# Four convolution layers on one core: the last three emitted in an explicit order, and loads and stores of the first moved

## The chip, the cores and the metric

The kernel runs on one core of a Trainium2 chip. The metric is the device time of the whole program in microseconds (us). Engines are named as in the profile: PE is TensorE (matmuls), DVE is VectorE, ACT is ScalarE, POOL is GpSimd, SP is SyncE; POOL and SP only issue DMAs here. A float32 matmul shows as two instructions ("passes") on PE.

## The reference, cut to what matters

The input has 32 images of 8 channels and 256 x 256 pixels in float32. Each of four layers adds to x a function of x that was normalized over 4 groups of channels.

```python
x = x + L0(gn(x))      # gn: mean and variance of each image over pairs of channels

def L0(x):
    grid = x
    for _ in range(15):
        mapped = 3.9 * grid * (1 - grid)
        local = conv3x3_per_channel(mapped, K_local)
        grid = 0.85 * (0.7 * mapped + 0.3 * local) + 0.15 * x
    cml = clip(grid, 1e-4, 1 - 1e-4)
    nca = sigmoid(conv1x1(relu(conv3x3(x, Wp, bp)), Wu, bu))          # 8 -> 128 -> 8
    g = sigmoid(conv1x1(relu(conv3x3([x, cml, nca], Wg1, bg1)), Wg2, bg2))   # 24 -> 8 -> 8
    return g * cml + (1 - g) * nca

x = x + conv3x3(quantized(gn(x)), quantized(w1)) / scales + b1   # scale: maximum over all images
x = x + conv3x3(gn(x), w2) + b2
x = x + conv5x5_per_channel(gn(x), w3)
```

## The kernel before, in words

**Two stages.** Layer 1 needs the largest value over the whole batch, so layer 0 is done for all 32 images first, and its sums go to memory (`x1_d`). Then layers 1 to 3 follow for all images.

**Layer 0** weaves two streams of instructions together by hand, inside `tc.manual_schedule()`, where every engine executes in the order in which the program emits (lines 661 to 677). The first stream, `lattice(b)` (L328), does the 15 steps for image b. Six of the eight channels are kept as patches of 16 x 8 pixels on partitions: a patch product and a ring product for the neighbours on PE (L389, L391), an addition on DVE (L400), a square on ACT (L418), and four DMAs that copy the ring (`spread`, L259). Two channels are done on DVE alone (`tap`, L338). A step has two halves of three channels each; the generator says by `yield` how much other work may lie beside each (`BLOCK`). After the last step the patches are turned back (L428), copied to `xb` (L431), and stored to `cr_d` by four GpSimd DMAs (L439).

The second stream, `gated()` (L484), works on the image before. In chunks n of two rows per partition (8 an image), it loads `im` (L501), multiplies (`ph`, L634), applies the rectifier (L639), multiplies into `pn` (L610) and takes the sigmoid to `nh` (L588). A chunk is four batches. A gate (L507) follows some batches later: it loads `xq`, `cq`, their halos and `xc` (L513, L476, L518), multiplies (L526, L534, L538, L543), combines on DVE (L556 to L559), and stores the sum (L564). `due` says in which batch a gate begins; each further piece of it comes one batch later. The driver at L668 takes pieces of `gated` while the lattice's `yield` leaves units for them, and never passes into the next image.

`errands(b)` (L266) holds the DMAs and statistics of the next image, one piece at the end of each half. All loads and stores but those of the rings, the strips and the constants are issued by GpSimd in one order. Statistics are means over partitions by small matmuls (`stats_parts`, L95: products at L104 and L111, copies at L105 and L112); in layer 0 their PSUM tiles come from `ps_c`, three buffers that the lattice uses too, and `held` keeps the gated ones out of the stretch in which a half holds all three. The pool `ps_a` (tag `ps`, three buffers) serves `ph`, `pq` and the transposes.

**Layers 1 to 3** (from L680) are emitted without a manual order: the scheduler of the language orders the instructions from the program's priorities and its own costs. The loop at L830 emits per round b a load of image b, layer 3 of image b-3, layer 2 of b-1, layer 1 of b. Layer 1 quantizes x to bfloat16 `qh` (L743, L704 to L706), copies two halo blocks to `qb` (L143), and makes eight chunks of three products and one with the halo (`conv3`, L726, L730), with ACT, an addition and `bn_stats` after each (L757 to L759). Layer 2 normalizes into `xh` (L765), copies its halo to `xb2`, and does the same in float32 (L774, L775); then it stores to `x3_d` by 16 DMAs (L779), takes statistics (with L133 for a broadcast by group) and loads `y` with rows on partitions (L789). Layer 3 normalizes into `xr` (L797), copies four boundary rows to `xr2` (L803), and for each of four channel pairs and two halves of the rows makes five products (L812), one with the halo (L816) and an addition (L821). The halo product has 128 output columns, of which only the two at the border between the halves are not zero.

Of the kernel before, what the change touches and what calls it, by code (L numbers as in the profile page):

```python
# [17 lines left out]
P = 128  # L18
# [30 lines left out]
BLOCK = 6.5  # L49
# [17 lines left out]
def kernel(  # L67
# [100 lines left out]
    with ExitStack() as es:  # L168
# [97 lines left out]
        def errands(b):  # L266
# [53 lines left out]
            for _ in stats_parts(ps_c, bn, st, gavg_sb, "psc"):  # L320
                yield
            yield

            ps = ps_c.tile([P, 512], F32, name="ps", tag="psc")
# [3 lines left out]
        def lattice(b, ahead):  # L328
# [23 lines left out]
            for t4 in range(TX // 4):  # L352
# [6 lines left out]
                if t4 == 0:  # L359
                    nc.vector.tensor_scalar(  # L360
                        xi, xi, st[:, 0:1], st[:, 1:2], ALU.subtract, ALU.mult
                    )
                if t4 == 1:
# [18 lines left out]
            for step in range(STEPS):  # L382
                for half in range(2):
# [30 lines left out]
                    held.append(half)  # L414
# [7 lines left out]
                    held.clear()  # L422
# [15 lines left out]
            for r in range(0, RB, 4):  # L438
                nc.gpsimd.dma_start(  # L439
                    window(  # L440
                        cr_d[b % 3], r // 4 * C * HB * WP,
                        [[WP, HB * CP], [4 * C * HB * WP, 4], [1, WP]],
                    ),
                    xb[0 : HB * CP, r : r + 4, :],
                )

            row = HB * WP
            for q in range(HB // RQ):
                for c in range(2):
# [7 lines left out]
                    )  # L457

# [22 lines left out]
        held = []  # L481
        place = [0]

        def gated():  # L484
# [22 lines left out]
            def gate(n, quarter):  # L507
# [10 lines left out]
                nc.gpsimd.dma_start(xc, xr_d[b % 3][:, k0 : k0 + 2, :])  # L518
                yield 0
# [49 lines left out]
                parts = stats_parts(ps_c, bn, st, gavr_sb, "psc")  # L569
                more = True  # L570
                while more:

                    if not held:
                        more = next(parts, parts) is None
                    yield 0
# [46 lines left out]
            for n in range(B * NCH):  # L622
# [4 lines left out]
                due.setdefault(batch + 6, []).append(gate(n, quarter))  # L627
# [33 lines left out]
        with tc.manual_schedule():  # L661
# [4 lines left out]
            for b in range(B):  # L666
# [7 lines left out]
                for _ in ahead:  # L674
                    pass
            for _ in rest:
# [3 lines left out]
    with ExitStack() as es:  # L680
# [10 lines left out]
        w3h_sb = const(wt, w3h, [72, 2, P], "w3h_sb")  # L691
# [48 lines left out]
        def layer1(b, x1):  # L740
            for k in range(4):
                t = two.tile([P, 1024], F32, name="tq")
                nc.vector.tensor_scalar(  # L743
                    t, x1[:, bass.ts(k, 1024)], stat1[:, b, 0:1], stat1[:, b, 1:2],
                    ALU.subtract, ALU.mult,
                )
                quantize(
                    qh[:, 4 * k : 4 * k + 4, 1 : 1 + W],
                    t.rearrange("p (r w) -> p r w", w=W), sc[:, 0:1],
                )  # L750
# [224 lines left out]
```

## Time and profile before

The median is 17658.94 us of three runs (17651.33 to 17685.45). The profiled execution spans 17639.8 us.

| part of the profiled execution | us |
|---|---|
| first lattice, alone (L346 of image 0 to L346 of image 1) | 351 |
| lattices 1 to 31, each beside the gated work of the image before | 434 each |
| gated work of the last image, alone, to its last product | about 255 |
| layers 1 to 3, from about 14120 us | about 3520 |
| PE busy, share of the span | 90% |
| DVE busy, share of the span | 66% |

A row of the waits names who waited, for what, the total in us, the number of times and the longest. A row of the timeline has start, duration, engine, line, operation, out<-in and the number merged; in brackets stand the idle time of the engine before it and what ended that. For PE the granted clock matters beside the busy time: at half clock a product takes twice as long and still counts as busy.

### The profile page before, as it was taken

The page shows a single profiled execution, that of the slowest core. Times are in us where ns is not written, and L with a number is a line of the kernel's source. Part 1 is how long each engine was busy: PE and PEld are TensorE (multiplying, and loading weights), DVE is VectorE, ACT ScalarE, POOL GpSimd, SP SyncE. Part 2 cuts the span into 40 slices and gives each one's busy share as a digit, 9 for nine tenths or more (in the row PEclk, how much of TensorE's full clock was granted, in tenths as well). Part 3 has the DMA queues.
Part 4 walks back from the last instruction along what each step waited for, and adds up shares of the span by engine and source line. Part 5 has one row for each costly group of instructions (what it writes and reads, how often), then busy time and mean ns, then how long its engine had stood idle before and what let it go on. Part 6 is the DMA issues. An engine that isn't in the chain of part 4 may idle for free. (4 is left out here: it accounts for less than half of the span.)

```text
span 17639.8 us, 136421 instructions
## 1 busy us (share of the span) xinstructions
PE 15897.8 (90%) x42888; PEld 6371.8 (36%) x42888; DVE 11656.2 (66%) x14652; ACT 5700.9 (32%) x8862; POOL 3931.1 (22%) x6419
## 2 busy tenths in 40 slices
PE   5999999999999999999999999999999977777777
PEld 2333333333333333333333333333333333333333
DVE  6677777777777777777777777777777444444443
ACT  2333333333333333333334333333333410000000
POOL 1222222222222222222222222222222211111111
PEclk7999999999999999999999999999999988888888
DMA  4666666666666666666666666666666644444443
GB/s 95 138 140 140 142 140 139 144 141 141 141 147 140 142 140 143 140 141 144 141 140 146 141 141 141 144 143 141 140 141 133 123 93 89 90 89 89 88 88 81
DMA packets 861103, 2275.97 MB, mean 129 GB/s; under 512 B 296788, under 2 KB 500628, under 8 KB 780388
## 3 DMA queue, kind: packets, MB, share of 16 engines
q0 software_dynamic: 507904, 1492.90, 40.1%
q1 hardware_dynamic: 352484, 774.34, 21.7%
q8 instruction: 350, 5.73, 0.2%
q14 instruction: 365, 2.99, 0.1%
HBM read 1078.68 MB, written 471.38 MB: 88 GB/s over the span
## 5 line engine op out<-in xcount | busy, mean ns | idle before, releaser
L338 DVE SCALAR_TENSOR_TENSOR acc<-strip,taps_sb,acc 128x1024 f32<-128x1024 f32 x3840 | 4929.8, 1284 | 120.4 <-DMA strip<-strip 0.3
L639 ACT ACTIVATE hh<-ph,bp_sb 128x512 f32<-128x512 f32 x4096 | 2763.8, 690 | 5899.1 <-PE ph L634 5839.5
L634 PE MATMUL ph<-im,wp_sb 72*128 72x512 f32 x8192 | 4256.7, 637 | 209.9 <-DMA im<-xn_d 178.8
L400 DVE SCALAR_TENSOR_TENSOR psc<-psc,flat 128x512 f32<-128x512 f32 x2880 | 1934.1, 695 | 3474.3 <-PE psc L391 3459.5
L389 PE MATMUL psc<-state,patch_sb 128*128 128x512 f32 x5760 | 2742.9, 612 | 104.9 <-ACT state L418 62.8
L391 PE MATMUL psc<-rings,ring_sb 80*128 80x512 f32 x5760 | 2641.7, 593 | 26.9 <-DMA rings<-state 26.9
L501 POOL DMA_DIRECT2D im<-xn_d x3072 | 1718.4, 564 | 3695.0 <-PE ph L634 3412.8
L634 PEld LDWEIGHTS ph<-im,wp_sb 72*128 72x128 f32 x8192 | 1542.7, 198 | 2479.2 <-issue 2049.3
L418 ACT ACTIVATE state<-psc,minus 128x512 f32<-128x512 f32 x2688 | 1672.9, 690 | 1423.1 <-DVE psc L400 1309.6
L389 PEld LDWEIGHTS psc<-state,patch_sb 128*128 128x128 f32 x5760 | 1095.4, 195 | 1660.7 <-issue 1312.1
L391 PEld LDWEIGHTS psc<-rings,ring_sb 80*128 80x128 f32 x5760 | 1094.5, 190 | 1425.9 <-issue 1411.7
L610 PE MATMUL pn<-hh,wu_sb 128*32 128x512 f32 x8192 | 1195.9, 642 | 0.6 <-ACT hh L639 0.6
L812 PE MATMUL psv<-xr,w_sb 128*128 128x512 f32 x2560 | 1162.6, 596 | 15.3 <-DVE xr L797 15.3
L526 PE MATMUL pg<-xq,wg_sb 128*128 128x512 f32 x1536 | 809.8, 669 | 276.0 <-DMA xq<-nr_d 276.0
L779 POOL DMA_DIRECT2D x_d<-x x512 | 353.7, 703 | 2612.9 <-DVE x L774 2402.5
L564 POOL DMA_DIRECT2D x_d<-xc x256 | 150.6, 588 | 3171.3 <-DVE xc L559 3154.0
L821 DVE TENSOR_TENSOR y<-psv,y 128x512 f32<-128x512 f32 x256 | 176.8, 691 | 881.9 <-PE psv L816 881.8
L115 ACT ACTIVATE u<-u 128x1 f32<-128x1 f32 x128 | 25.9, 202 | 2264.7 <-DVE u L112 2264.0
L526 PE MATMUL pg<-cq,wg_sb 128*128 128x512 f32 x1536 | 748.9, 626 | 0.0
L726 PE MATMUL psv<-xh,w_sb 128*128 128x512 f32 x1536 | 706.7, 597 | 8.1 <-DVE xh L765 4.1
L812 PEld LDWEIGHTS psv<-xr,w_sb 128*128 128x128 f32 x2560 | 480.5, 190 | 599.9 <-issue 592.1
L338 DVE SCALAR_TENSOR_TENSOR acc<-strip,taps_sb,d 128x1024 f32<-128x1024 f32 x480 | 612.3, 1276 | 0.0
(163 smaller groups left out, 12766.2 us busy)
## 6 DMA issues: line engine op xcount, KB each, us to landing
im<-xn_d POOLq DMA_DIRECT2D x3072, 193.3 KB, 7.8
rings<-state SPq DMA_DIRECT2D x1920, 159.5 KB
rings<-state SPq DMA_DIRECT2D x1920, 106.3 KB
strip<-strip SPq DMA_DIRECT2D x960, 126.0 KB
xn_d<-xb POOLq DMA_DIRECT2D x128, 516.0 KB, 9.0
nr_d<-xb POOLq DMA_DIRECT2D x128, 516.0 KB, 9.8
xq<-nr_d POOLq DMA_DIRECT2D x128, 516.0 KB, 13.3
cq<-cr_d POOLq DMA_DIRECT2D x128, 516.0 KB, 16.1
```

The source lines that it names most:

```text
L338: nc.vector.scalar_tensor_tensor(acc, strip[:, dy : dy + RQ, dx : dx + W], taps_sb[:, 3 * dy + dx : 3 * dy + dx + 1], d2 if dy == 1 and dx ...
L389: nc.tensor.matmul(pss[-1], patch_sb[:, c, :], inner(c), start=True, stop=False)
L391: nc.tensor.matmul(pss[c % HALF], ring_sb[:, c, :], rings[half][:, c % HALF, 0 : TX * SY].rearrange("p (x y) -> p x y", y=SY)[:, :, 0:TY], ...
L400: nc.vector.scalar_tensor_tensor(ps, ps, FLOOR, dr[:, c], ALU.max, ALU.add)
L418: nc.scalar.activation(inner(c), pss[c % HALF], AF.Square, bias=minus)
L501: nc.gpsimd.dma_start(im[24 * dy : 24 * dy + 24, k, 0:run], window(xn_d[b % 3], at, [[HP * WP, C], [1, 3], [1, run]]),)
L526: nc.tensor.matmul(o, wg1_sb[:, s, dx, :], src[:, :, dx : dx + W], start=s == dx == 0, stop=False,)
L610: nc.tensor.matmul(pn[32 * q : 32 * q + 32, :], wu_sb[:, i, :], hh, start=i == 0, stop=i == 3,)
L634: nc.tensor.matmul(ph.rearrange("p (k w) -> p k w", w=W), wp_sb, im[:, :, j * WP : j * WP + W], start=True, stop=True,)
L639: nc.scalar.activation(hh, ph, AF.Relu, bias=bp_sb)
L726: nc.tensor.matmul(o, w[:, dx, :], src[:, 2 * i : 2 * i + 2, dx : dx + W], start=dx == 0, stop=False,)
L812: nc.tensor.matmul(o, w3_sb[:, dx, :], xr[:, k, 2 * g : 2 * g + 2, dx : dx + W], start=dx == 0, stop=False,)
```

## The change

In layers 1 to 3 the order is now written out inside `tc.manual_schedule()`. The layers become generators that give up control after each chunk, and `among` puts small tasks between the chunks. In round b: among layer 3 of image b-3 lie the last statistics of layer 1, normalizing and halo for layer 2 of b-1, and quantizing and halo for layer 1 of b; among layer 2 of b-1 lies normalizing for layer 3 of b-2; among layer 1 of b lie the statistics of layer 2. The point is that each layer's products are preceded by prepared inputs. Layer 3's halo product now has 32 output columns, for the half and the block of partitions that need it, and those of the two halves are emitted one after the other.

In layer 0 the stores of `cr_d` move from the end of a lattice into the next one, a gate's loads begin a batch earlier while its products stay where they were (a second empty `yield`), the statistics' tiles move to the pool `ps_a` and `held` is gone, and `BLOCK` falls from 6.5 to 6.3.

```diff
-BLOCK = 6.5
+BLOCK = 6.3
...
-            for _ in stats_parts(ps_c, bn, st, gavg_sb, "psc"):
+            for _ in stats_parts(psum, bn, st, gavg_sb, "ps"):
...
-            ps = ps_c.tile([P, 512], F32, name="ps", tag="psc")
+            ps = psum.tile([P, 512], F32, name="ps")
             nc.tensor.matmul(ps[:, 0:2], pick_sb, st, start=True, stop=True)
...
+                if t4 == 4 and b > 0:
+                    store(b - 1)
...
-                    held.append(half)
                     yield 1.7
...
-                    held.clear()
                     next(ahead, None)
...
-            for r in range(0, RB, 4):
-                nc.gpsimd.dma_start(
-                    window(
-                        cr_d[b % 3], r // 4 * C * HB * WP,
...
+        def store(b):
+            xb = xbs[b % 2]
+            for r in range(0, RB, 4):
+                nc.gpsimd.dma_start(
+                    window(
+                        cr_d[b % 3], r // 4 * C * HB * WP,
...
                 nc.gpsimd.dma_start(xc, xr_d[b % 3][:, k0 : k0 + 2, :])
                 yield 0
+                yield 0
...
-                parts = stats_parts(ps_c, bn, st, gavr_sb, "psc")
-                more = True
-                while more:
-                    if not held:
-                        more = next(parts, parts) is None
+                for _ in stats_parts(psum, bn, st, gavr_sb, "ps"):
                     yield 0
...
-                due.setdefault(batch + 6, []).append(gate(n, quarter))
+                due.setdefault(batch + 5, []).append(gate(n, quarter))
...
+            store(B - 1)
             for _ in rest:
                 pass
...
-        w3h_sb = const(wt, w3h, [72, 2, P], "w3h_sb")
+        w3h_sb = const(wt, w3h, [72, 2, 32], "w3h_sb")
...
+        def layer3(b, y):
             for g in range(4):
...
                 for k in range(2):
-                    ps = ps_v.tile([P, 512], F32, name="psv")
-                    o = ps.rearrange("p (c w) -> p c w", w=W)
-                    for dx in range(5):
...
+                    pss.append(ps_v.tile([P, 512], F32, name="psv"))
+                    for dx in range(4):
+                        last(k, dx, False)
+                    if k == 0:
+                        yield
+                for k, at in ((0, P - 32), (1, 0)):
                     nc.tensor.matmul(
-                        o, w3h_sb[:, k, :], xr2[:, 2 * g : 2 * g + 2, 0:W],
-                        start=False, stop=True,
-                    )
+                        pss[k][at : at + 32].rearrange("p (c w) -> p c w", w=W), w3h_sb[:, k, :],
+                        xr2[:, mine, 0:W], start=False, stop=False,
+                    )
+                for k in range(2):
+                    last(k, 4, True)
...
-        for b in range(B + 3):
-            if b < B:
-                x1 = load1(b)
-            if b >= 3:
-                layer3(b - 3, *threes.pop(b - 3))
-            if 1 <= b <= B:
-                threes[b - 1] = layer2(b - 1, *twos.pop(b - 1))
-            if b < B:
-                twos[b] = layer1(b, x1)
+        with tc.manual_schedule():
+            x1s[0] = load1(0)
+            for b in range(B + 3):
+                if b + 1 < B:
+                    x1s[b + 1] = load1(b + 1)
+                tasks = {i: [] for i in range(8)}
+                if 1 <= b <= B:
+                    st, parts = sums.pop(1)
+                    for i in range(4):
+                        tasks[i].append(step(parts))
+                    tasks[3].append(lambda: normal2(x2s[b - 1], st))
+                if b < B:
+                    for k, i in enumerate((0, 1, 2, 4)):
+                        tasks[i].append(lambda k=k: quantize1(b, x1s[b], k))
+                    tasks[5].append(lambda: beside(nc.sync, qb, qh, 0))
+                among(layer3(b - 3, ys.pop(b - 3)) if b >= 3 else iter(()), tasks)
+                tasks = {}
+                if 2 <= b <= B + 1:
+                    for g in range(4):
+                        tasks[g] = [lambda g=g: normal3(ys[b - 2], gss[b - 2], g)]
+                    tasks[3].append(beside3)
...
+                among(layer2(b - 1, x2s[b - 1], bn2) if 1 <= b <= B else iter(()), tasks)
+                tasks = {}
+                if 1 <= b <= B:
+                    st3, parts3 = begin(bn2)
+                    for i in range(4):
+                        tasks[i + 1] = [step(parts3)]
...
+                    tasks[6] = [groups]
+                    ys[b - 1] = load3(b - 1)
...
+                among(layer1(b, x1s[b], x2s[b], bn1) if b < B else iter(()), tasks)
+                if b < B:
+                    sums[1] = begin(bn1)
```

## The prediction

> **What bounds the kernel now.** I read the page first, for the stages.
>
> ```profile
> PE 15897.8 (90%) x42888; PEld 6371.8 (36%) x42888; DVE 11656.2 (66%) x14652; ACT 5700.9 (32%) x8862; POOL 3931.1 (22%) x6419
> ...
> PE   5999999999999999999999999999999977777777
> ...
> PEclk7999999999999999999999999999999988888888
> ```
>
> TensorE carries both stages, more tightly in layer 0 (32 slices) than in layers 1 to 3 (the last 8). The view of windows puts numbers on one stretch of each; its columns are busy time by engine, then granted clock, DMA share and GB/s.
>
> ```profile
> 8000.00:10000.00 2000.00, 1900.08 (x5304) 751.57 (x5303) 1474.86 (x1720) 784.20 (x1230) 502.07 (x838) 0.95 0.68 141
> 15000.00:16000.00 1000.00, 765.24 (x1859) 331.15 (x1858) 412.63 (x784) 91.49 (x126) 120.13 (x171) 0.86 0.41 88
> ```
>
> So what can be won is TensorE idle time, and the clock lost with it. Layer 0 first: TensorE's waits between 2000 and 13500 us, some 26.5 images.
>
> ```profile
> PE pg L526 <- DMA xq<-nr_d: 226.0, 26, 9.6
> PE ph L634 <- DMA im<-xn_d: 129.7, 24, 7.1
> PE ps L104 <- ACT state L418: 72.0, 53, 1.4
> ```
>
> The first two come once per image, 8.7 and 5.4 us. One image in TensorE's timeline, then what GpSimd did just before each wait:
>
> ```profile
> 6060.81 1.04 PE L355 MATMUL ps<-eye_sb,flat 128*128 128x128 f32 x8
> 6068.97 3.75 PE L634 MATMUL ph<-im,wp_sb 72*128 72x512 f32 x4 [7.12 <-DMA im<-xn_d]
> ...
> 6138.88 1.98 PE L634 MATMUL ph<-im,wp_sb 72*128 72x512 f32 x4
> 6149.99 4.87 PE L526 MATMUL pg<-xq,wg_sb 128*128 128x512 f32 x6 [9.12 <-DMA xq<-nr_d]
> ```
>
> ```profile
> 6046.87 6.11 POOL L439 DMA_DIRECT2D cr_d<-xb  x4 [10.95 <-DVE xb L431]
> ...
> 6126.57 0.59 POOL L564 DMA_DIRECT2D x_d<-xc  x1 [31.20 <-DVE xc L559]
> ...
> 6129.48 2.19 POOL L501 DMA_DIRECT2D im<-xn_d  x4
> 6134.75 0.60 POOL L513 DMA_DIRECT2D xq<-nr_d  x1 [3.07 <-DMA xn_d<-xb]
> ```
>
> First wait: GpSimd stood 10.95 us at the cr_d stores until VectorE had copied xb, then issued for 6.11 us, and the image loads queued behind. Second: the xq load is issued 8.2 us after GpSimd is released by L564, six im loads ahead of it, and it lands 15 us later. A group of four ph passes takes 3.75 us after the stop against 1.98 us otherwise: the clock is halved. In windows of 10 us the clock reads 0.50 from 6070 to 6090 and 0.87 in the next. Layer 0's clock of 0.95 is 5%, about 22 us of each image's 434 (L346 starts 32 times, first at 34.6 us, last at 13422.8); some 4 of these fall into the waits themselves. The loss is 22 us idle (all waits of that window, about 590 us) and 18 us of half speed; undisturbed, an image would take 434 - 40 = 394 us.
>
> Layers 1 to 3, one round of TensorE:
>
> ```profile
> 15241.10 1.02 PE L730 MATMUL psv<-xb,w_sb 72*128 72x512 f32 x2
> 15244.10 0.58 PE L104 MATMUL ps<-mv,gavr_sb 128*128 128x1 f32 x2 [1.98 <-DVE mv L101]
> 15245.52 0.59 PE L111 MATMUL ps<-t,gavr_sb 128*128 128x1 f32 x2 [0.84 <-DVE t L108]
> 15247.83 0.59 PE L133 MATMUL ps<-sel,ones 128*128 128x8 f32 x2 [1.72 <-DVE sel L131]
> 15253.23 5.70 PE L726 MATMUL psv<-qh,w_bf 128*128 128x512 bf16 x15 [4.80 <-ACT qh L706]
> 15276.33 2.31 PE L730 MATMUL psv<-qb,w_bf 72*128 72x512 bf16 x5 [17.39 <-DMA qb<-qh]
> ```
>
> Layer 2 runs from 15214.46 to 15242.0 without a gap (27.5 us), layer 1 with its waits to 15282.47 (40.5), layer 3 to 15324.30 (41.8): 110 us a round. Layer 1's own 32 bf16 passes are 7 us at the spacing that they show once warm (0.22). The rest of its stretch is a serial chain: statistics of layer 2, quantizing, and 17.4 us for the halo of qh.
>
> **What the Trainium skill says.** *TensorE: Matmul & The Clock Gate*, section "What's actually happening": the clock falls to half after an idle window of about 3.4 us and comes back after about as long a busy one. The trace agrees on the halving; return took 4 us after the 9.12 us wait but about 25 us after the 7.12 us one, so I count clock loss from the trace. The same page, "Architectural detail", calls ScalarE, VectorE and GpSimd strict FIFO, with TensorE moving only weight loads ahead: the GpSimd rows show that. *TensorEngine Tiling (Array Packing)*, "Key Properties": tiles on different partitions compute in parallel. Layer 0's own pair agrees: above and below (L534) start at 6128.98 and 6128.98, two passes each, and L538 follows at 6129.96, 0.98 us for the four.
>
> **The change, part by part.** *Layer 3's halo.* Eight full halo products a round (two passes of 0.43 us, L816 to the next L812: 0.86 us) become four pairs of 32-column products at 0.98: 6.9 - 3.9 = 3.0 us saved. Layer 3 takes 8 x 4.30 (ten L812 passes) + 3.9 + 0.5 for two statistics products = 38.8 us.
>
> *Rounds.* Statistics of layer 1, normalizing, quantizing and both halos now lie inside layer 3. VectorE's work there (8 x 0.69 adds, 4 x 2.24 quantizing, 2.4, about 2 of small ones) is 19 us, inside 39. The xh halo is issued about 23 us into layer 3 and needed at 41 (38.8 + 2.6 of layer 2): 18 us. The trace doesn't show its least duration; the bounds are 7.8 us (what an im load of 193 KB takes to land) and the 17.4 that qb took beside stores, so I count no wait and carry 0 to 4 us. The qb halo has 40 us. Layer 2 stays at 27.5.
>
> *Layer 1's stretch* becomes VectorE's. From layer 2's end: last add, bn_stats and aggregate end at +2.1 (as at 15244.04). Eight chunks at 0.68 + 0.68 plus gaps are 1.44 each, 11.5; statistics pieces among them 2.0; by_group 0.45, then TensorE must answer (0.7) before the copy and the eighth chunk. TensorE waits for the sums at slot 2 (t ready at +5.8) and at slot 6 for sel (+14.7); it issues the last chunk at +15.3, at half clock 1.7 us: 17.0 us. Behind it queues layer 3, which starts cold; I add 2.5 us. Round: 38.8 + 27.5 + 17.0 + 2.5 = 85.8, against 110: 24 us saved. Over 29 full rounds 700; the thinner first and last rounds keep their length within some 20: take 690. Bounds 500 (xh wait of 4, a longer cold start) to 800.
>
> *Layer 0, stores.* The cr_d stores go from the lattice's end to the fifth transpose of the next lattice, when L431 is long done: the 10.95 us of standing goes. The 6.1 us of issue and 1.5 MB of traffic remain, now ahead of the next half's loads, which have roughly 14 us of slack against 3.3 of issue and 7.8 of landing: about 1.5 us stays. Saves 4 us an image (bounds 0 to 5.4).
>
> *Gate loads a batch earlier, the product where it was* (second empty yield). xq goes ahead of six im loads (3.3 us) and of the 3.07 us wait behind them, so it is issued about 7 us earlier: of 8.7 us, 1.7 stay. Saves 7 (4 to 8.7).
>
> *Statistics in the ps pool.* The waits for state L418 (72 + 37.5 + 36.7 us over the window, 5.4 us an image) go. In return the third ph after such a product finds the buffer held until VectorE's copy: of the five products of the image at 6046, the copies end before the third ph in four; only the gated one (product 6197.9, copy until 6204.3) would hold it some 3 us. Net saving 2.5 (-3 to 5).
>
> *BLOCK 6.5 to 6.3.* Lattice gaps go from 229 to 223 units (5+8+9+4+30 x BLOCK+8), the gated work of an image being 223. Both streams still sum to the same TensorE work: nothing, but for the 1.5 us of L428 waits.
>
> *Clock.* With both long stops gone most of the 18 us of half speed goes; shorter stops can still trigger it (a 1.36 us one at 6196 was followed by 0.56 for 10 us). I take 12 saved (4 to 16). Sum: 4 + 7 + 2.5 + 12 = 25.5 us an image, x 31 = 790.
>
> Total: 17658.94 - 690 - 790 = 16180; I say 16200.
>
> **Rivals.** (a) *The stops move*: stores and loads collide at the new place, and clock loss stays. For it: DMA share is 0.9 to 1.0 around 6050 to 6070, the same stretch. Layer 0 then saves about 8 us an image: 17659 - 690 - 250 = 16720. (b) *Layers 1 to 3 stay bound by waits*: the fixed order makes TensorE stand for VectorE's small results and for the xh halo, a round of 98 us: 350 + 790 saved, 16520. Against it: VectorE has idle time for all this (0.41 busy). (c) *Layer 0 runs clean* at 394 us: 40 x 31 + 690, 15730. (d) *Slower*: held ps buffers stop TensorE five times an image for 5 us, half clock for 20 more, +45 x 31 = 1400 less 690 saved: about 18400. Against it: the copies' times above.
>
> **How the numbers follow.** Forecast 0.50, (a) 0.17, (b) 0.14, (c) 0.13, (d) 0.05; something that cancels, 0.01. Range 15800 to 16800: it takes in (a) and (b) and the upper part of the unknowns, and leaves out (d) and most of (c). Faster 0.94, same 0.01, slower 0.05.
>
> **What would show it.** Right: L346 starts every 405 to 412 us; TensorE's waits on im and xq under 2 us an image; no long stop at L439's successor; layer 2 to layer 2 in 84 to 88 us, no wait on qb, and TensorE waiting at L104, L111 and L133 inside layer 1. Wrong: the ph wait turning up against VectorE's st or u copies; a wait of L730 on xb; clock below 0.95 in either stage.

## The result and the profile after

| | us | ratio to before (95% interval) |
|---|---|---|
| before | 17655.14, median beside these runs | |
| after | 16890.31 (16850.15 to 16911.87, four runs) | 0.9561 (0.954 to 0.9583) |

The forecast of 16200 us had the direction right and the size wrong: about 765 us were saved where 1460 were forecast, and 16890 lies above its range. The profiled executions take 17639.8 and 16909.8 us, 730 less. At the last start of L346 (the last image's lattice) they part: it comes at 13373.6 us against 13422.8, 49 us earlier, and from there to the end it takes 3536.2 us against 4217.0, 681 less. That stretch still holds the last lattice and its gated work; from the first product of layer 1 to the end the traces show 2827.4 us against 3489.7, so layers 1 to 3 themselves saved 662. For these the forecast said 690; for layer 0 it said 790. (The 49 is at the low end: two kernels below with the same layer 0, full_halo and s2_stats, reach that start at 13320.4 and 13300.9 us.)

The page of after, first the busy times, then the slices:

```profile
PE 15762.1 (93%) x42888; PEld 6291.4 (37%) x42888; DVE 11707.7 (69%) x14652; ACT 5744.5 (34%) x8862; POOL 3820.6 (23%) x6419
...
PE   5999999999999999999999999999999997999999
...
PEclk7999999999999999999999999999999998999999
```

The last slices have changed from 7 to 9 for TensorE and from 8 to 9 for its clock; nothing is to be seen in the first 32. The view of windows, with the same stretches as before:

```profile
8000.00:10000.00 2000.00, 1899.69 (x5271) 753.50 (x5269) 1460.77 (x1702) 779.64 (x1218) 490.66 (x837) 0.95 0.68 140
15000.00:16000.00 1000.00, 924.66 (x2368) 382.99 (x2367) 546.84 (x1017) 128.04 (x168) 143.84 (x228) 0.94 0.51 114
```

Layer 0 has the same busy time (1899.69 us of 2000 against 1900.08), the same clock and the same DMA share. L346 starts every 433.5 us, before every 433.9 (mean from the third start to the last). Yet the waits are others. TensorE's waits from 2000 to 13000 us, 25.4 images:

```profile
PE ph L633 <- ACT hh L638: 211.7, 103, 4.9
PE psc L393 <- DMA rings<-state: 118.6, 53, 5.9
PE ph L633 <- DMA im<-xn_d: 103.3, 17, 7.6
PE ph L633 <- DVE xb L431: 49.5, 26, 1.9
```

The wait on xq, first before with 226 us, and the one on state L418 are gone. The wait on im fell little: before it was 118.9 us in this stretch, and 48.0 us more of the waits at the same product now stand under other DMAs that landed last. In place of the others stand 8.3 us an image for the rectifier (L638), 4.7 for the lattice's rings, and 1.9 for the copy of xb. The timeline shows the image from 6060 us again, a little later in its own course:

```profile
6067.23 5.46 PE L393 MATMUL psc<-rings,ring_sb 80*128 80x512 f32 x6 [5.56 <-DMA rings<-state]
...
6105.36 2.08 PE L633 MATMUL ph<-im,wp_sb 72*128 72x512 f32 x2 [3.15 <-ACT hh L638]
...
6239.60 3.75 PE L633 MATMUL ph<-im,wp_sb 72*128 72x512 f32 x4 [4.90 <-DMA im<-xn_d]
```

At the head of the image, where TensorE stood 7.12 us for im, it now stands 5.56 us for the rings. In before the ring products of this image came only at 6096.95, 28 us after the im wait, and did not wait. The second row is the new kind of stop. The third is the im wait at a new place. Around the second row, ScalarE:

```profile
6102.85 1.89 ACT L419 ACTIVATE state<-psc,minus 128x512 f32<-128x512 f32 x3 [10.56 <-DVE psc L402]
6104.63 1.84 ACT L638 ACTIVATE hh<-ph,bp_sb 128x512 f32<-128x512 f32 x3
```

and VectorE in the same microseconds:

```profile
6087.65 7.88 DVE L338 SCALAR_TENSOR_TENSOR acc<-strip,taps_sb,acc 128x1024 f32<-128x1024 f32 x6
...
6097.43 0.69 DVE L560 TENSOR_TENSOR cq<-cq,nh 128x512 f32<-128x512 f32 x1
...
6102.12 1.89 DVE L402 SCALAR_TENSOR_TENSOR psc<-psc,flat 128x512 f32<-128x512 f32 x3
```

VectorE has a second half's six taps (7.88 us) and two small instructions to do, then a gate's combination and its statistics (L560 to L567, seven instructions of about 0.69), and only then the additions (L402) of the next half. ScalarE has the squares (L419) that need those additions at the head of its queue and stands 10.56 us; the rectifiers behind them start 0.1 us before the squares end; TensorE has no free `ph` buffer until then. Now GpSimd, ahead of the im wait at 6239.60:

```profile
6205.88 0.60 POOL L568 DMA_DIRECT2D x_d<-xc  x1 [13.29 <-DVE xc L563]
...
6216.60 0.56 POOL L504 DMA_DIRECT2D im<-xn_d  x1 [2.30 <-DMA xq<-nr_d]
...
6221.11 0.82 POOL L296 DMA_DIRECT2D nr_d<-xb  x1 [3.94 <-DMA cq<-cr_d]
```

GpSimd stood 13.29 us at the store of a gate's sums until VectorE had made xc, then issued the gate's loads, and the im loads came behind these, the last at 6231.70, with waits in between, most of them for landings, that add up to 14 us. That is the pattern of before with xq and im exchanged.

Layers 1 to 3 follow the forecast's picture. One round of TensorE:

```profile
15270.08 1.02 PE L730 MATMUL psv<-xb,w_sb 72*128 72x512 f32 x2
15273.08 0.38 PE L104 MATMUL ps<-mv,gavr_sb 128*128 128x1 f32 x2 [0.24 <-DVE mv L101]
15276.39 0.38 PE L111 MATMUL ps<-t,gavr_sb 128*128 128x1 f32 x2 [2.04 <-DVE t L108]
15286.06 0.59 PE L133 MATMUL ps<-sel,ones 128*128 128x8 f32 x2 [4.11 <-DVE sel L131]
```

Layer 3 runs from 15202.58 to 15243.45 (40.9 us), layer 2 to 15270.94 (27.5), layer 1 with its waits to 15288.17 (17.2): a round of 85.6 us. The waits on qb (17.39 us) and qh (4.80) are gone; what stops TensorE is L104, L111 and L133 inside layer 1.

### The profile page after: what moved, and what is told of

Same layout as the page of the kernel before. It is cut to its first block, busy times and chain, and to the rows that moved or that the text cites. A ratio compares the mean times of both kernels' runs of the same rounds, so it can differ in the third digit from the quotient of the medians.

```text
span 16909.8 us, 135970 instructions
## 1 busy us (share of the span) xinstructions
PE 15762.1 (93%) x42888; PEld 6291.4 (37%) x42888; DVE 11707.7 (69%) x14652; ACT 5744.5 (34%) x8862; POOL 3820.6 (23%) x6419
## 5 line engine op out<-in xcount | busy, mean ns | idle before, releaser
L638 ACT ACTIVATE hh<-ph,bp_sb 128x512 f32<-128x512 f32 x4096 | 2764.0, 691 | 4873.6 <-PE ph L633 4818.6
L402 DVE SCALAR_TENSOR_TENSOR psc<-psc,flat 128x512 f32<-128x512 f32 x2880 | 1935.6, 696 | 3256.2 <-PE psc L393 3236.6
L391 PE MATMUL psc<-state,patch_sb 128*128 128x512 f32 x5760 | 2844.8, 632 | 74.5 <-ACT state L419 63.7
L393 PE MATMUL psc<-rings,ring_sb 80*128 80x512 f32 x5760 | 2727.2, 610 | 176.4 <-DMA rings<-state 176.0
L419 ACT ACTIVATE state<-psc,minus 128x512 f32<-128x512 f32 x2688 | 1690.9, 691 | 1816.3 <-DVE psc L402 1750.7
L391 PEld LDWEIGHTS psc<-state,patch_sb 128*128 128x128 f32 x5760 | 1131.5, 202 | 1730.3 <-issue 1411.0
L812 PE MATMUL psv<-xr,w_sb 128*128 128x512 f32 x2560 | 1200.6, 619 | 1.3 <-DVE xr L793 1.3
L777 POOL DMA_DIRECT2D x_d<-x x512 | 304.2, 610 | 2115.5 <-DVE x L771 1854.0
L530 PE MATMUL pg<-xq,wg_sb 128*128 128x512 f32 x1536 | 759.0, 633 | 0.0
L755 ACT ACTIVATE x<-psv,b_sb,sc 128x512 f32<-128x512 f32 x256 | 199.8, 780 | 1598.2 <-PE psv L730 1592.7
L480 POOL DMA_DIRECT2D below<-nh x288 | 197.3, 685 | 1860.5 <-ACT nh L587 1860.5
```

The costliest lines, as they stand in the source:

```text
L391: nc.tensor.matmul(pss[-1], patch_sb[:, c, :], inner(c), start=True, stop=False)
L393: nc.tensor.matmul(pss[c % HALF], ring_sb[:, c, :], rings[half][:, c % HALF, 0 : TX * SY].rearrange("p (x y) -> p x y", y=SY)[:, :, 0:TY], ...
L402: nc.vector.scalar_tensor_tensor(ps, ps, FLOOR, dr[:, c], ALU.max, ALU.add)
L419: nc.scalar.activation(inner(c), pss[c % HALF], AF.Square, bias=minus)
L530: nc.tensor.matmul(o, wg1_sb[:, s, dx, :], src[:, :, dx : dx + W], start=s == dx == 0, stop=False,)
L638: nc.scalar.activation(hh, ph, AF.Relu, bias=bp_sb)
```

## The experiments

Each time below is the median of four runs, each interval is that of the ratio to before measured beside them; a tenth of a per cent is 18 us. "Period" is the mean time between starts of L346 in the profile, from the third to the last; "rest" is the time from its last start to the end. For the same stretch the period can be taken apart: idle time is the period less TensorE's busy time; half of the busy time for which the clock record reads 0.50 is lost to the clock; what is left came to 392 us in every profile, from 391.6 to 392.7. Before has 22.3 us idle and 19.0 lost to the clock, after 21.8 and 19.5. Profiles of the same layer 0 differ by about 1 us in the one and 1.5 in the other.

### What each edit of layer 0 is worth

The theory: the edits that the forecast valued do work, but something else hides their gain. The rival: some of them cost time by themselves. One kernel keeps layers 1 to 3 of after and takes layer 0 of before; the others take one edit out of after. The diff of the change shows these edits; here only the part put back is given.

All four edits undone:

> Layer 0 as before, layers 1 to 3 as after. By the two traces the whole gain lies in layers 1 to 3 (681 us of the span after the last lattice start). Theory A (layer 0's edits gave nothing): 16975 us, within 40, a ratio of 0.9615. Rival (layer 0's edits gave some gain which the profiled run hides, or cost some): more than 60 us away from 16975 on either side.

Measured: 16998 us, 0.9621 (0.9607 to 0.9636), period 434.7, rest 3547.6. So layers 1 to 3 by themselves bring some 660 us, and the four edits of layer 0 together about 107, 3.5 us an image instead of 25.5. The time lies within the 40 us that were given to the theory of no gain, but its interval and that of after (0.954 to 0.9583) don't meet: the gain is small, not nothing.

The stores back at the lattice's end (the same `store`, emitted after the last copy):

```diff
-                if t4 == 4 and b > 0:
-                    store(b - 1)
...
                 yield 1
+            store(b)
```

> After with the cr_d stores at the end of the lattice, as before. Theory A: the im wait of 5 to 7 us at the lattice's head comes back with slow clock after it and the rings wait at the head (4.7 us an image) goes, since it was hidden behind the other; 16890 plus 50 to 250. Rival: within 30 us of 16890, one stop in place of the other.

Measured: 17117 us, 0.9692 (0.9678 to 0.9707), period 439.1. TensorE's wait on im rises from 4.1 to 7.0 us an image, and the one on the rings falls from 4.7 to 1.1. Over 11000 us TensorE is busy for as long as in after, but at a lower clock, and gets fewer passes done. First after, then this kernel:

```profile
2000.00:13000.00 11000.00, 10445.84 (x28915) 4141.00 (x28914) 8067.15 (x9399) 4286.69 (x6685) 2699.36 (x4592) 0.95 0.69 141
...
2000.00:13000.00 11000.00, 10452.44 (x28497) 4118.72 (x28497) 7979.27 (x9293) 4222.00 (x6587) 2715.52 (x4532) 0.93 0.68 140
```

Moving the stores saves 227 us, 7.3 an image, and none of it is idle time: that is 21.8 us an image in both. The loss to the clock is 25.6 us here and 19.5 in after. Between 2000 and 12500 us the clock record has 16 stretches of 27.3 us at half clock here, as in before, and none above 20.5 us in after.

The statistics back in `ps_c`, held back by `held` (all of layer 0; the cut shows the gated ones):

```diff
-                for _ in stats_parts(psum, bn, st, gavr_sb, "ps"):
+                parts = stats_parts(ps_c, bn, st, gavr_sb, "psc")
+                more = True
+                while more:
+                    if not held:
+                        more = next(parts, parts) is None
                     yield 0
```

> After with layer 0's statistics in ps_c and held again, nothing else. The forecast took 2.5 us an image for this edit. Theory A (it saves the waits for state, 5.5 us an image, and slow clock after them): those waits return and the time is 16890 plus 60 to 250. Rival (a held ps buffer costs as much as the waits did, and helps to make the ph stops of 8.3 us): the ph stops shrink by 3 us or more and the time is 16890 or less.

Measured: 17226 us, 0.9754 (0.9727 to 0.9781), period 441.8. The lattice's products now wait for the statistics' copies, L112 and L105, 6.0 us an image. The pool is worth about 336 us by the times (266 by the profiled executions), 8 to 11 an image; 2.2 of these are idle time. The rectifier's wait is 3.6 us an image here, not 8.3. The rival had expected that, but with a shorter time. Of the rectifier's two long stops in an image one is gone, and at its place, by the same gate's combination, stands the wait on L112, 3.9 us once an image.

The gate's loads back where they were:

```diff
                 yield 0
-                yield 0
...
-                due.setdefault(batch + 5, []).append(gate(n, quarter))
+                due.setdefault(batch + 6, []).append(gate(n, quarter))
```

> After with a gate's loads a batch later and one empty yield, as before. Theory A: the xq wait of about 8 us an image comes back; the im wait in the middle of an image (4.9 us, behind the gate's loads in GpSimd's order) goes or halves; net 16890 plus 0 to 150. Rival (the pace is set elsewhere): within 30 us of 16890.

Measured: 16716 us, 0.9463 (0.9446 to 0.948), period 427.7: without this edit the kernel is 174 us faster. The expectation was 0 to 150 us slower. The wait on im is gone, and xq, loaded late, costs 1.6 us an image, not the 8.5 of before. Its waits are the rectifier's (8.2 us an image, as in after) and the rings' (5.8).

`BLOCK` back at 6.5:

```diff
-BLOCK = 6.3
+BLOCK = 6.5
```

> After with BLOCK 6.5 again, nothing else. Theory A (the new stops come from how gates and lattice halves fall against each other: a gate's VectorE work after the six taps holds the squares, ScalarE stands at them, ph fills its buffers): the phase shifts, so the 8.2 us an image of ph waiting on ScalarE change by more than 3 us, and the time by 30 to 200 us, either way. Rival (the stops only show a pace that the lattice's chain sets, whatever the order): the waits change places but an image still takes 434 us within 2, the total within 30 us of 16890.

Measured: 16754 us, 0.949 (0.9476 to 0.9504), period 427.1: 137 us faster. Its waits of TensorE:

```profile
PE ph L633 <- DMA im<-xn_d: 220.3, 19, 15.3
...
PE ph L633 <- ACT hh L638: 14.8, 52, 0.4
```

The rectifier's wait is down to 0.6 us an image, and the one on im has doubled to 8.5 (in both kernels more of it stands under other DMAs). TensorE's idle time is about the same, 22.1 us an image against 21.8, but it lies in long stops, and the loss to the clock is 13.2 us against 19.5: there are 81 stretches at half clock between 2000 and 12500 us, against 124 in after. So two of the four edits cost time in the kernel after, and the rival holds for them: early gate loads and `BLOCK` 6.3. Both were undone together:

> After with BLOCK 6.5 and the gate's loads of before: of the four edits of layer 0 the stores and the statistics stay. Theory A (each of the two cost its own stop: BLOCK 6.3 the wait on ScalarE, the early gate loads the wait on im): both go, xq stays at 1.5 us an image since the stores' place cured it, and the time is 16450 to 16620. Rival (one stop takes the place of the other): 16700 or more.

Measured: 16549 us, 0.9371 (0.9352 to 0.9391), 341 less than after; one by one they gave 174 and 137. The two don't hide each other. But the wait on xq is back at its old size, though it had been expected to stay at 1.5 us an image:

```profile
PE pg L529 <- DMA xq<-nr_d: 229.5, 26, 10.6
```

With the gate loads at +6, then, it is `BLOCK` that decides over this wait: 1.6 us an image at 6.3, 8.8 at 6.5. And the early gate loads cost time at either setting, 174 us at 6.3 and 204 at 6.5 (16754 against 16549).

### Why TensorE waits for the rectifier

The theory: a gate's combination lies on VectorE between a second half's taps and the next first half's additions, and through ScalarE's queue holds the rectifiers. The rival: the statistics in `ps` hold the `ph` buffers, which the forecast had feared. To the kernel with gate loads at +6 was added only this: a combination that would come right after a second half waits a batch.

```diff
+                    turn[0] = half
                     yield 1.7
...
+            turn[0] = 0
             for t4 in range(TX // 4):
...
                 yield 0.9
+                if turn[0] == 1:
+                    yield 0
```

> l0_gate6 (16716 us) with one more edit: a gate's combination on VectorE is put off by a batch when it would follow a second half, with its six taps. Theory A (combination after six taps holds the additions of the next first half, ScalarE's squares wait for these ahead of the rectifiers, and ph has no free buffer): the 8.2 us an image of ph waiting on ScalarE fall below 3, and with the clock the time falls by 150 to 400 to about 16450. Rival (ps buffers are held by the statistics): the 8.2 us stay within 1.5 us and the time within 60 us of 16716.

Measured: 16376 us, 0.9281 (0.926 to 0.9302), period 414.4, 340 less than without them.

```profile
PE ph L637 <- ACT hh L642: 19.5, 76, 0.4
```

The rectifier's wait is 0.7 us an image instead of 8.2, with the statistics still in `ps`. The theory holds for this wait, and the rival falls. Other waits moved too: the rings' went from 5.8 to 3.4, and 3.2 us came for im and xb, so 340 us is the net of all of these. What `BLOCK` did is less simple. By the order in the traces four of an image's eight combinations come behind a second half at 6.3, and three at 6.5. In after only two of the four, the second and the seventh, make ScalarE stand for long (10.6 and 10.4 us), and these are TensorE's two stops of 3.2 and 4.5 us; at 6.5 ScalarE stands 2.0 to 2.8 us behind such a combination, and TensorE isn't stopped. So the place behind a second half isn't enough for a stop: rectifiers that TensorE needs must lie behind those squares. Why they do at 6.3 and not at 6.5 wasn't worked out.

### Why loads of xq or im come late

Two theories. One: it is a matter of the order of loads and `cr_d` stores. The other: GpSimd stands at the store of a gate's sums, and what follows comes as a burst, of which some load is always late. First, the former. Starting from b65_g6 the cr_d stores were put behind the first ring copies of the next lattice, out of the stretch where the DMA engines are fullest:

```diff
-                if t4 == 4 and b > 0:
-                    store(b - 1)
...
                         spread(half)
+                        if step == half == 0 and b > 0:
+                            store(b - 1)
```

> As b65_g6, and the cr_d stores wait until the ring copies of the first step's first half are issued. Theory A (the wait on rings of 5 to 7 us an image at the lattice's head comes from the stores' traffic in front of the ring copies): it falls below 2 us, time 100 to 250 below b65_g6. Rival (the ring copies are issued too late by ScalarE whatever is on the queues): the wait stays, time within 60 us of b65_g6, or an im wait takes its place.

Measured: 16320 us, 0.9241 (0.9226 to 0.9256), 229 less; the rings' wait falls from 6.5 to 4.0 us an image, not below 2 as expected, and the one on xq from 8.8 to 5.2. To this kernel was added an early load for the first gate of an image only, whose xq was the late one; and to that, the move of statistics in layers 1 to 3 that is described below:

```diff
                 yield 0
+                if r2 == 0 and b > 0:
+                    yield 0
...
-                due.setdefault(batch + 6, []).append(gate(n, quarter))
+                early = n % NCH == 0 and n > 0
+                due.setdefault(batch + (5 if early else 6), []).append(gate(n, quarter))
```

> b65_g6_step (16320 us) with only the first gate of each image loading a batch early, products where they were. Theory A (its remaining xq wait of 5.6 us an image is GpSimd's order: six im loads ahead of the first gate's): the wait falls below 2 us, time 16130 to 16230. Rival (the load waits for the cr_d stores or for VectorE's combination ahead of it): the wait stays above 4 us, within 60 us of 16320.

> best_l0 and s2_stats together. Theory A (the two stages do not touch): the savings add, best_l0 less what s2_stats saves on after, 15850 to 15980. Rival: 16050 or more.

Measured: 16404 us (0.9286, 0.9269 to 0.9302) and 16186 us (0.9158, 0.9141 to 0.9175). The xq wait is gone, as expected, but the time of the first is 84 us longer, since im is late instead, by up to 16.5 us:

```profile
PE ph L635 <- DMA im<-xn_d: 102.6, 10, 16.5
```

In best_all the moved statistics bring 218 us, near the 226 that they bring on after. An early load alone fails. Now the other theory, tried on after itself: the gate loads stay early, the product stays where it was, and the store of the sums is emitted a batch later. (xc is loaded a batch later, so that its two buffers still do.)

```diff
+                yield 0
                 xc = hp.tile([P, 2, W], F32, name="xc", bufs=2)
                 nc.gpsimd.dma_start(xc, xr_d[b % 3][:, k0 : k0 + 2, :])
                 yield 0
-                yield 0
...
+                yield 0
                 nc.gpsimd.dma_start(x1_d[b][:, bass.ts(r2, 512)], flat)
```

> After with the store of a gate's sums emitted a batch later (and xc loaded at its old batch, which the buffers need). Theory A (GpSimd standing at that store is what makes the early gate loads and the im loads compete): im waits of layer 0 fall from about 6 to below 2 us an image, time 16600 to 16750. Rival (too many loads in the queue): im waits stay above 4 us, time 16830 or more.

Measured: 16464 us, 0.9325 (0.9303 to 0.9346), period 418.8: 426 less than after. All of TensorE's larger waits from 2000 to 13000 us:

```profile
PE ph L634 <- ACT hh L639: 219.0, 131, 4.5
PE psc L393 <- DMA rings<-state: 74.9, 30, 6.0
PE ph L634 <- DVE xb L431: 51.5, 27, 1.9
```

No im and no xq; the rectifier's wait is untouched at 8.3 us an image, as it must be. The gain is larger than expected (16600 to 16750). Two of GpSimd's rows, in the image that starts at 5818.8 us; the store comes 178 us after that start, as the one at 6205.88 did in after:

```profile
5984.94 0.56 POOL L516 DMA_DIRECT2D xq<-nr_d  x1
...
5997.41 0.59 POOL L569 DMA_DIRECT2D x_d<-xc  x1 [5.56 <-DVE xc L563]
```

The gate's loads now go out ahead of the stand, and the im loads come right behind the store. So it is the place of this store in GpSimd's order that made im late. The stand itself has not gone: GpSimd stands for xc 2101.9 us in the window against 3028.1 in after. Whether the shorter stand or the loads' place ahead of it counts more was not separated, and neither was the later load of xc.

The same store, on b65_g6_step:

> b65_g6_step (16320 us) with the same later store. Theory A: its xq wait of 5.6 us an image falls below 2, time 16130 to 16230. Rival: the wait stays above 4 us or an im wait of its size comes, 16280 or more.

Measured: 16222 us, 0.9188 (0.9168 to 0.9209), 98 less. The time is as expected; the xq wait falls from 5.2 to 2.8 us an image, not below 2: with late loads it helps less, presumably because the load itself is issued late (not tried). The rings' wait grew from 4.0 to 5.1.

### Layers 1 to 3

Layer 3's halo with 128 output columns again:

```diff
-        w3h_sb = const(wt, w3h, [72, 2, 32], "w3h_sb")
+        w3h_sb = const(wt, w3h, [72, 2, P], "w3h_sb")
...
-                for k, at in ((0, P - 32), (1, 0)):
+                for k in range(2):
                     nc.tensor.matmul(
-                        pss[k][at : at + 32].rearrange("p (c w) -> p c w", w=W), w3h_sb[:, k, :],
+                        pss[k].rearrange("p (c w) -> p c w", w=W), w3h_sb[:, k, :],
```

> After with layer 3's halo products over all 128 columns again. Theory A (the forecast's term): 3.0 us more a round, 32 rounds, 96 us: 16985. Rival (changing between 32 and 128 columns costs TensorE what the shorter work saves, or the time hides beside other waits): within 40 us of 16890.

Measured: 16945 us, 0.9595 (0.9565 to 0.9625). The interval overlaps with that of after (0.954 to 0.9583), so the times leave it unclear. In the profile the rest grows by 75.5 us, from 3536.2 to 3611.7; from the first product of layer 1 on it is 66.0 us, 2.1 a round, where the forecast said 3.0.

Then the waits at L104, L111 and L133. The theory: they set layer 1's stretch, because layer 2's statistics can only be worked on while TensorE has but 7 us of layer 1 to do. The rival: VectorE's chunks (1.44 us each) set it, and the waits only name the last arrival. The statistics were moved among the next round's layer 3, where TensorE has 39 us of work, their last step to the start of layer 2, and layer 3's normalizing and layer 1's statistics a slot on:

```diff
-                    for i in range(4):
+                    for i in (1, 2, 3, 3):
                         tasks[i].append(step(parts))
...
+                if 2 <= b <= B + 1:
+                    st3, parts3 = sums.pop(2)
+                    for i in range(4, 8):
+                        tasks[i].append(step(parts3))
...
+                    def groups():
+                        gss[b - 2] = by_group(psum, st3)
+
+                    tasks[0] = [groups]
...
-                    st3, parts3 = begin(bn2)
-                    for i in range(4):
-                        tasks[i + 1] = [step(parts3)]
...
-                    tasks[6] = [groups]
+                    sums[2] = begin(bn2)
```

> After with the statistics of layer 2 taken out of layer 1's stretch and laid among the next round's layer 3. Theory A (layer 1's 17.2 us are TensorE standing for VectorE's small results, 6.3 us of waits at L104, L111 and L133, and half clock after them): the stretch falls to 7 to 9 us, a round by 8 to 11 us, the time to 16540 to 16640. Rival (VectorE's 11.5 us of additions and bn_stats hold the PSUM buffers, so layer 3's first products wait instead): less than 3 us a round, 16800 or more.

Measured: 16664 us, 0.9427 (0.9412 to 0.9442), 226 less than after; in the profile the rest falls to 3330.2, and a round from 85.6 to 78.4 us. The time is 24 us above what was expected (16540 to 16640). Layer 1's stretch is 7.0 us, TensorE's own time: the theory holds. But 4.0 of its 10.2 us come back at the start of layer 2, which takes 31.5 us instead of 27.5, behind the wait at L133 and at half clock. What is left of those waits from 14300 to 16300 us:

```profile
PE ps L133 <- DVE sel L131: 47.6, 26, 1.8
```

### Put together

> b65_g6_step with s2_stats. Theory A (the stages' savings add): 16320 less 226, 16094 within 50. Rival: 16180 or more.

> step_defer with s2_stats. Theory A: step_defer less 226, 15900 to 16010. Rival: 16050 or more.

> after_defer with BLOCK 6.5 and s2_stats: early gate loads, sums stored a batch later, cr_d stores at the fifth transpose. Theory A (phase of the halves and stand at the store are separate causes): no ph wait on ScalarE above 1 us an image, no im and no xq wait above 1, some rings wait at the lattice's head; 15950 to 16080. Rival (BLOCK 6.5 brings the im waits back, as in l0_block65): im above 4 us an image, 16150 or more.

> The same with the cr_d stores behind the first ring copies (the gates of image 0 load a batch later than the others, since the stores must come before). Theory A: as early_defer_s2 without most of the rings wait at the head, 20 to 100 us less, and at least 40 us less than step_defer_s2 (16023). Rival (the early loads only move the wait to im or rings): 16020 or more.

| stores of cr_d | gate loads | sums' store | us | ratio (95% interval) | period | rest |
|---|---|---|---|---|---|---|
| behind ring copies | +6 | at once | 16099 | 0.9117 (0.9099 to 0.9136) | 412.7 | 3313.1 |
| behind ring copies | +6 | a batch later | 16023 | 0.9075 (0.9055 to 0.9094) | 410.8 | 3310.7 |
| in the lattice's head | +5 | a batch later | 15890 | 0.9006 (0.8985 to 0.9028) | 404.9 | 3310.5 |
| behind ring copies | +5 | a batch later | 15933 | 0.9031 (0.9009 to 0.9054) | 406.9 | 3297.7 |

All four have `BLOCK` 6.5, statistics in `ps`, and layer 2's statistics in layer 3. (In the last one image 0's gates stay at +6.) The first came out as expected, the second 13 us above its range and the third 60 us below; the fourth was to be 20 to 100 us below the third and is 43 above it. The third, the kernel after with `BLOCK` 6.5, the deferred store and the moved statistics, is the fastest, 1000 us below after. TensorE is busy for 96% of it. Its largest wait from 2000 to 12500 us, 25.9 images:

```profile
PE psc L393 <- DMA rings<-state: 133.0, 62, 7.5
```

All other waits there are below 0.9 us each, and none is for im or xq. Early gate loads, which cost 174 us in after, belong to the fastest kernel: with the store of the sums behind them, they make xq early and nothing late. The second and the fourth row, which differ by the gate loads alone but for image 0, show 90 us. What is left is the rings' wait at an image's head, 5.1 us. Moving the stores behind the ring copies had eased it in b65_g6_step; here it brought nothing (the intervals of the last two rows overlap). What that wait is made of stays open.

## Why the prediction was wrong

**Layers 1 to 3, right in mechanism and size.** Forecast 85.8 us a round, measured 85.6: layer 3 40.9 (38.8, and part of the 2.5 for a cold start), layer 2 27.5 (27.5), layer 1's stretch 17.2 (17.0). The sum was 690; the profile shows 662 in these layers. There is no wait on the xh or qb halo, and the stops are at L104, L111 and L133, as the forecast named them. The halo's term, 3.0, measured 2.1 when undone.

**Layer 0, the failing step: the sum "4 + 7 + 2.5 + 12 = 25.5 us an image".** It took each wait as removed by its own edit, with nothing in its place, and the clock as following. The three waits were to take 13.5 us of idle time from an image; TensorE's idle time fell by 0.5, from 22.3 to 21.8. The clock was to give 12 us; the loss to it went from 19.0 to 19.5. Measured with one edit undone at a time, in us an image:

| step | forecast | measured, all in all | idle time, by profile | clock, by profile |
|---|---|---|---|---|
| stores moved | saves 4 | saves 7.3 | nothing | saves 6.2 |
| statistics in `ps` | saves 2.5 | saves 8 to 11 | saves 2.2 | saves 5.9 |
| gate loads a batch earlier | saves 7 | costs 5.6 | costs 3.2 | costs 2.9 |
| `BLOCK` 6.3 | nothing | costs 4.4 | saves 0.4 | costs 6.3 |
| clock | saves 12 | contained in the others | | |
| all | saves 25.5 | saves 0.4 (period) to 3.5 (times) | saves 0.5 | costs 0.5 |

The rows don't add up to the last: what an edit is worth depends on what stands beside it.

The stores' term counted on 4 us less idle time. GpSimd's stand at these stores did go, but the rings' wait took the place of im's, and what the move saved came from the clock. The statistics' term was right in mechanism, and for the idle time in size: their waits are gone from after, and come back when the edit is undone. The forecast's fear for them, held `ps` buffers against the st or u copies, did not show. The forecast gives its waits of 8.7 and 5.4 us as means of one wait; per image they are 8.5 and 4.9.

"Gate loads a batch earlier" read the rows ahead of the xq wait as six im loads in its way. It left out the row above them, in the same fence: GpSimd standing 31.20 us at L564 for VectorE's xc, with all these loads behind it. With that store left ahead of them an earlier xq only changes which load is late, as best_l0 showed again (xq gone, im up to 16.5 us). The store a batch later saved 426 us. And in after there was little left for the early loads to save: with them undone the wait on xq was 1.6 us an image. *DMA: Bandwidth & Descriptors* in the Trainium skill, section "Rules for kernel authors", advises to issue a DMA early and wait for it late. The runs agree only under a condition: where the loads share one issuing order with a store that waits ahead of them, the early issue cost 174 us; with that store behind them it is part of the fastest kernel.

"`BLOCK` 6.5 to 6.3 … nothing" reasoned from TensorE's work alone. The setting also decides how a gate's combination on VectorE and the rectifiers on ScalarE fall against the halves of the lattice. At 6.3 two combinations in an image, between a second half's taps and the next additions, make most of the 8.3 us an image that TensorE waits for the rectifier. Its idle time as a whole was the same at 6.5; the many short stops cost more of the clock than fewer long ones. The forecast had not worked out VectorE's order in layer 0 at all.

"Clock, 12" followed from "both long stops gone", and stops did not go. Halving needs no stop of 7 us: the wait of 5.56 us on the rings was enough (ring products 5.46 us afterwards, 2.74 when warm). In the fastest kernel an image loses 7.5 us idle and 5.5 to the clock, and takes 404.9 us. So the forecast's "undisturbed image" of 394 us was a good floor (392 by the profiles); the change didn't reach it.

Of the rivals, (a), the stops move, 16720 us, named the kind of failure and came nearest, in part by its own cause: it spoke of stores and loads colliding at the new place of the stores. That move was among the gains, but the stores do stand in the way of the ring copies there: behind these they cost 229 us less in b65_g6_step, though nothing less in the fastest kernels.

## What to carry to other kernels

Where several waits alternate on one engine, look for what the engines behind them stand at, and cost an edit only if it removes that; otherwise count on the next wait in line. Keep idle time and the loss to the clock apart when an edit is costed: here two edits left the first as it was and moved the second by 6 us an image, one up and one down. In an order written by hand, put a DMA store that waits for a compute engine behind the loads that don't, before any load is moved earlier. And put an engine's optional work where the next instruction on which another engine's queue depends isn't waiting for it.

## What the runs showed of the hardware

- After a stop the length of the half-clock stretch didn't follow the stop's length: about 24 us after the 7.12 us stop of before, about 4 us after its 9.12 us one. In the clock records of before, after, l0_store_end, l0_block65, after_defer and the fastest kernel every stretch at half clock between 2000 and 12500 us lasts 3.4 us or a multiple of it, up to 27.3. The clock's share of a change couldn't be worked out from its waits alone.
- Short stops matter together: a wait of 1.36 us was followed by a clock of 0.56 for 10 us in before. With the same idle time of about 22 us an image, 124 stretches at half clock (after) cost 19.5 us an image, 81 (l0_block65) 13.2.
- A GpSimd load can wait for the landing of an earlier, unrelated one: the xq load of before at 6134.75 waited 3.07 us for an xn_d store, which fits the one issued eight DMAs earlier; b65_g6_step shows the same distance at 11608.69, and in after the store at 6221.11 waited for the cq load eight DMAs before it. Whether this comes from the language's semaphores or from the chip was not tried.
